# Moving first-norm statistics from attention into the convolution stages, and lending three heads in place of two to accumulating transfers

## The chip, the cores and the metric

The kernel runs on one core of one Trainium2 chip. The metric is the device time of one execution in microseconds (us). Names of engines: PE is the matrix engine (PEld its weight loads), DVE the vector engine, ACT the activation engine, POOL the general-purpose engine, SP the engine that only issues transfers. Each engine works through its own instructions in order, and waits on semaphores for the others.

## What is computed

Four images of 256 channels and 48 x 48 pixels pass two layers in fp32. Cut to what matters:

```python
def layer0(x):                     # x: (4, 256, 48, 48)
    y = relu(batchnorm(conv3x3(group_norm(x))))          # "first norm" is this group_norm
    q, k, v = split(einsum('oc,bchw->bohw', qkv_w, y))   # 8 heads of 32 channels, N = 2304 tokens
    attn = softmax(einsum('bhdn,bhdm->bhnm', q, k) * 32 ** -0.5)
    return x + proj(einsum('bhem,bhnm->bhen', v, attn))

def layer1(x):
    g = group_norm(x)                                    # second norm
    w = conv3x3(g, 45 maps)                              # 5 dilations x 9 taps, softmax over taps
    cat = [g] + [sum_taps(g shifted by dilation d, weighted by w) for d in (1, 6, 12, 24, 36)]
    return x + batchnorm_over_batch(conv1x1(cat))
```

A group norm needs the mean and the variance of each group of 8 channels over the whole image before any of it can be normalized.

## The kernel before

**Stages.** An image's 256 channels are two halves of 128 partitions. The loop over `b` from 0 to 4 makes one round per image: the convolution with q, k and v of image `b` (`conv_qkv`), side by side with the dynamic filters (layer 1) of image `b - 1` (`dynamic_filters`), and then attention of image `b` (`attention`). So the time line is: convolution of image 0 alone, attention 0, filters 0 with convolution 1, attention 1, filters 1 with convolution 2, attention 2, filters 2 with convolution 3, attention 3, filters 3 alone, the end. In the shared stages a planner with a cost clock (`clock`, `fill`, `run`) decides at build time how the matmuls of the two are interleaved; in attention the order is written out by hand. The order of the program on each engine is fixed.

**Attention.** It goes over 9 units of queries (eight of 512 queries of one half, that is 4 heads each, and a ninth that takes the last 256 queries of both halves), and in each unit over 18 key blocks `m` of 128 keys. In one step (`scores`, L954 to L963) PE makes the scores of 4 heads, one into a PSUM tile `so` with one buffer and three into `se` with two, and ACT takes their exponentials into a tile `p` of 4 x 512 numbers per partition (L962 one head, L963 three). In the next step (`weigh`) PE multiplies `p` with v into `num` (L983), and the sum of `p` over the key blocks is kept in `acc`, from which the denominator is made in `close` two units later (L1015, L1024, L1026, L1027, L1034). `p` has four buffers: the exponential of step m + 4 must wait until everything that reads `p` of step m is done.

**Lent key blocks.** The sum is DVE's (L999, all four heads). In units 1 to 8, in the steps m of `LENT = (2, 5, 8, 11, 14)` (the last unit leaves out 14), DVE adds two heads only, and POOL issues a transfer of the other two from `p` into `extra`, a slice of the tile `scratch`: a plain copy for m = 2 (L1001), and one that adds to what is there for the others (L1003). Each of these transfers waits for the one before. At the unit's last step (m = 15 in the last unit) DVE adds `extra` to `acc` (L1006). The tile `scratch` is 1536 numbers wide, of which 1024 are used.

**Projections.** In step 6 of units 3, 5, 7 and 8 finished parts of the attention output are projected (`project`, L1069, and L1078 and L605 on DVE), one part of six in units 3, 5 and 8, two in unit 7, the sixth after attention. `project` writes a tile `pp` of the same PSUM pool as `se`.

**Statistics of the next image.** The class `Norm` makes them in three parts: `part` is one `bn_stats` of DVE (L605) for each of 12 pieces; `finish` is a generator: first `bn_aggr` (L614), then a small matmul (L617), a copy and two squares on ACT (L618, L620), then two more matmuls (L627, L628) and `rstd_of` (DVE L87, a square root on ACT L88, DVE L89); `shift_of` is one DVE instruction (L634). Exponential and square root are in different tables of ACT, so a square root costs two table loads, there and back. `stats_of` loads the 12 pieces of image `b + 1` by SP (`xst`, L1516) and calls `part`; it is advanced by `merged` within the convolution of image `b`. The three parts of `finish` are in a list `spare`, called by attention of image `b` in step 2 of unit 1 and just ahead of the projections of units 3 and 5, with the third bank of `pp` for the small matmuls. Behind them in `spare` are three calls that normalize image `b + 1` in place (12 instructions of ACT, L1734, in three groups of 4): two calls in unit 7, one in unit 8.

Of the kernel before, what the change touches and what calls it, by code (L numbers as in the profile page):

```python
# [33 lines left out]
QC = 512  # L34
# [14 lines left out]
def conv_preact_kernel(  # L49
# [482 lines left out]
    with tc.tile_pool(name="w", bufs=1) as wpool, tc.tile_pool(  # L532
# [394 lines left out]
        def attention(b, q, k_, vT, pools, spare, project, scratch):  # L927
# [4 lines left out]
            zeros = work0.tile([P, D], F32, tag="zeros", name=f"zeros_{b}", bufs=1)  # L932
            nc.gpsimd.memset(zeros, 0.0)

            extra = scratch[:, : 2 * QC].rearrange("p (j n) -> p j n", j=2)
            scratch = work0.tile([P, QC], F32, tag="rt", name=f"rt_{b}", bufs=1)

            whole, rest = N // QC * QC, N % QC
# [30 lines left out]
            def weigh(u, m, p):  # L969
                if m == 0:  # L970
                    state[u] = dict(
                        num=ps_a.tile([P, 512], F32, tag="num", name=f"num_{b}_{u}"),
                        acc=work0.tile([P, 4, QC], F32, tag="acc", name=f"acc_{b}_{u}"),
                    )
                st = state[u]
                several = len(units[u]) > 1
                if several and m == 0:

                    for j, r in enumerate(heads):
                        nc.tensor.matmul(st["num"][r, :], zeros, p[:, j, :], start=True, stop=False)  # L980
                for i, (g, q0, n, at) in enumerate(units[u]):
                    for j, r in enumerate(heads):
                        nc.tensor.matmul(  # L983
                            st["num"][r, at : at + n],
                            vT[:, m, g * P + j * D : g * P + (j + 1) * D],
                            p[:, j, at : at + n],
                            start=(m == 0 and not several),
                            stop=(m == NT - 1 and i == len(units[u]) - 1),
                        )
                end = u == last  # L990
                if end and m == NT - 1:
                    sums(u, p, True, False)
                elif m == 0:
                    st["first"] = p
                else:
                    other = st["first"] if m == 1 else st["acc"]
                    lend = u > 0 and m in LENT[: len(LENT) - end]
                    js = slice(0, 2 if lend else 4)
                    nc.vector.tensor_tensor(st["acc"][:, js], other[:, js], p[:, js], ALU.add)  # L999
                    if lend and m == LENT[0]:  # L1000
                        nc.gpsimd.dma_start(out=extra, in_=p[:, 2:])  # L1001
                    elif lend:
                        nc.gpsimd.dma_start(out=extra, in_=p[:, 2:], accum_op=ALU.add)  # L1003
                if u and m == (NT - 3 if end else NT - 1):
                    rest = st["acc"][:, 2:]
                    nc.vector.tensor_tensor(rest, rest, extra, ALU.add)  # L1006
                if m == NT - 1 and not end:
                    g, q0, n, _ = units[u][0]
                    nc.scalar.copy(ao[:, g, q0 : q0 + n], st["num"])
# [29 lines left out]
            for i, (u, m) in enumerate(steps):  # L1039
                ps = scores(u, m)  # L1040


                if m == 1 and u > 1:
                    close(u - 2)
                if prev is not None:
                    weigh(*steps[i - 1], prev)
                prev = ps
                if m == 2 and u == last:
                    close(u - 1)
                if m == 6 and (u % NH == 1 or u == last):  # L1050
                    while (chunk + 1) * CH <= units[u if u == last else u - 1][0][1]:
                        pp = three(f"pp_{b}_{chunk}")
                        if spare:
                            spare.pop(0)(pp[:, 2, :])
                        project(chunk, ao, pp)
                        chunk += 1
                if m == 2 and u == 1 and spare:
                    spare.pop(0)(None)
            assert not spare
            weigh(*steps[-1], prev)  # L1060
            close(last)
# [42 lines left out]
            for _, _, _, y0, y1, x0, x1 in taps_of(c, n)  # L1104
        )

        def dynamic_filters(b, ao, chunk, norm, other, pools):


            ps_w, ps_y, ps_m, work1 = pools  # L1110
# [6 lines left out]
            def run(ns):  # L1117

                while ns > 0:
                    got = next(other, None)  # L1120
                    if got is None:
                        return
                    spent[0] += got
                    ns -= got
# [98 lines left out]
            ready = {}  # L1223


            while chunk < NCK:
                project(b, chunk, ao, ps_y.tile([P, 2, 512], F32, tag="y", name=f"pp_{b}_{chunk}"), norm)
                chunk += 1
            table(AF.Sqrt)
            run(2400)  # L1230
            for at, _ in enumerate(norm.finish(misc)):
                run((600, 700)[at])
            table(AF.Exp)

            for r0, r1 in ((0, 2 * R + 1), (2 * R + 1, HH)):
# [348 lines left out]
                    nc.sync.dma_start(out=image_of(out, b)[:, :, cols], in_=ty[c])  # L1584

        u_next = None
        for b in range(B + 1):

            with tc.tile_pool(name=f"work1_{b}", bufs=2) as work1, tc.tile_pool(
# [11 lines left out]
                if b < B:  # L1601
                    weights, between = taken, ()
                    if b == 0:
                        wc = work1.tile([P, NH, 9, C], F32, tag="wc", name="wc", bufs=1)
                        for h in range(NH):
                            nc.gpsimd.dma_start(out=wc[:, h], in_=conv_w[:, h])
                        nc.gpsimd.dma_start(out=wqkv, in_=qkv_w)
                        nc.gpsimd.dma_start(out=wp, in_=proj_w)
                        nc.gpsimd.dma_start(out=vbc, in_=v_b.rearrange("(h p) -> p h", p=P))
                        nc.gpsimd.dma_start(out=wcat, in_=cat_w)  # L1610
                        nc.gpsimd.dma_start(out=wsc, in_=scale_w)
                        weights = Made(wc, work1)
                        rest = norm0.finish(psc)
                        next(rest)
                        weights.pair(ORDER[0], [0], weights.home)
                        for _ in rest:
                            pass
                        norm0.shift_of()
                        def rows(r0, r1):
                            for h in range(NH):  # L1620
                                to, of = (
                                    inside(pads[0], h, r0, r1 - r0),
                                    rows_of(x_first[:, h, :])[:, r0:r1, :],
                                )
                                if h:
                                    nc.scalar.activation(
                                        to, of, AF.Identity, bias=norm0.shift[:, h : h + 1],
                                        scale=norm0.rstd[:, h : h + 1],
                                    )
                                else:  # L1630
                                    normalize(to, of, norm0.mean, norm0.rstd, h)


                        rows(0, HH // 2 + 2)
                        weights.pair(ORDER[0], [1], weights.home)
                        between = (
                            lambda: rows(HH // 2 + 2, HH),
                            lambda: weights.pair(3, range(NH), weights.other),
                        )
                        u_next = weights(ORDER[0])  # L1640
                    nn, stats = None, iter(())
                    if b + 1 < B:
                        nn = Norm("n0", b + 1)
                        stats = stats_of(b + 1, work1, nn)
                    other = merged(
                        conv_qkv(b, pads[b % 2], psc, weights, u_next, work1, between), 40000.0,
                        4000.0, stats,
                    )
                if b == 0:
                    for j, _ in enumerate(other):  # L1650
# [15 lines left out]
                else:  # L1666
# [31 lines left out]
                            for c, t in enumerate(y_2):  # L1698
                                nc.sync.dma_start(out=t, in_=chunk_of(y_d, 2, c))

                    dynamic_filters(b - 1, ao, chunk, norm1, other, (ps_w, ps_y, ps_m, work1))
                    if b == B:
                        finish(work1)
            if b == B:
# [13 lines left out]
            if b + 1 < B:  # L1718
                load_pad(b + 1)
                u_next = taken(ORDER[0])  # L1720
                bank = [None]
                fin = nn.finish(lambda name, bank=bank: bank[0])

                def stats(t, nn=nn, bank=bank, fin=fin):
                    bank[0] = t
                    if next(fin, fin) is fin:
                        nn.shift_of()

                todo = [(h, r0) for h in range(NH) for r0 in range(0, HH, R)]

                def pieces(_, some, b=b, nn=nn):
                    for h, r0 in some:
                        t = inside(pads[(b + 1) % 2], h, r0, R)
                        nc.scalar.activation(  # L1734
# [1 line left out]
                            scale=nn.rstd[:, h : h + 1],  # L1736
                        )

                spare = [stats] * 3 + [
                    lambda t, some=todo[i::3], f=pieces: f(t, some) for i in range(3)  # L1740
                ]
            norm1 = Norm("n1", b)
            q, k_, vT = qkv[b]
            with tc.tile_pool(name=f"work0_{b}", bufs=2) as work0, tc.tile_pool(
# [81 lines left out]
```

## Time and profile before

| | us |
|---|---|
| median of 3 runs (lowest, highest) | 2887.96 (2886.28, 2889.66) |
| the profiled execution | 2887.44 |
| its span, first to last instruction | 2885.7 |
| convolution of image 0, up to the first exponential | 0 to 145.3 |
| exponentials of attention 0, 1, 2, 3 (first and last start) | 145.3 to 511.8, 836.7 to 1204.7, 1529.6 to 1897.1, 2217.3 to 2580.9 |
| busy PE, DVE, ACT, POOL | 2726.2, 2445.6, 1677.0, 1190.2 |
| granted PE clock, mean | 0.979 |

A row of the groups names a line of the code, the engine, the operation, what is written and read, how often, the busy time in all, the mean of one, and then the time for which the engine stood idle just before such instructions, with what ended the wait. A row of the timeline gives start, duration, engine, line and operation, and in brackets the idle time before. L962 starts each step of attention, so the distance between two starts of L962 is the length of a step.

### The profile page before, as it was taken

Reading aid. Unit: us, or ns where it says so; the run is one execution under the profiler, and the core shown is the slowest. Engines: PE = TensorE matmul, PEld = TensorE weight load, DVE = VectorE, ACT = ScalarE, POOL = GpSimd, SP = SyncE. Lnnn points to the kernel's source line nnn. Section 1 sums busy time; section 2 is a strip of 40 time slices with the busy share of each in tenths; the row PEclk is TensorE's granted clock in tenths of the full one; section 3 lists DMA queues with packets and bytes.
Section 4 is the critical chain, followed back from the end, with each engine's and each line's share of the span. In section 5 each row is a group of like instructions: output and inputs, shape, how many; then the busy total and the mean of one; then the engine's idle time right before and its main releaser. Section 6 shows DMA issues by size and latency. Waiting matters only on the chain. (4 is left out here: it accounts for less than half of the span.)

```text
span 2885.7 us, 43628 instructions
## 1 busy us (share of the span) xinstructions
PE 2726.2 (94%) x16950; PEld 1202.4 (42%) x16950; DVE 2445.6 (85%) x2570; ACT 1677.0 (58%) x2107; POOL 1190.2 (41%) x1000
## 2 busy tenths in 40 slices
PE   7999999999999999999899999999999999998994
PEld 5722224556542222456562222356555222244562
DVE  6489999789879989878887998978886999987886
ACT  3398988322359889712237988842234988861224
POOL 1000000898840000299791010069986011006893
PEclk9999999999999999999999999999999999999997
DMA  4413333122242233223224333323213133325225
GB/s 179 104 31 71 67 65 82 44 89 87 68 104 64 65 72 76 61 64 95 68 68 99 67 72 72 70 55 87 69 50 77 45 72 76 73 50 222 60 70 207
DMA packets 148199, 232.04 MB, mean 80 GB/s; under 512 B 66760, under 2 KB 117008, under 8 KB 146192
## 3 DMA queue, kind: packets, MB, share of 16 engines
q0 software_dynamic: 23264, 87.21, 13.5%
q1 hardware_dynamic: 82384, 87.31, 10.7%
q10 hardware_dynamic: 42336, 54.66, 7.0%
q8 instruction: 135, 2.21, 0.3%
q14 instruction: 80, 0.66, 0.1%
HBM read 115.02 MB, written 32.33 MB: 51 GB/s over the span
## 5 line engine op out<-in xcount | busy, mean ns | idle before, releaser
L999 DVE TENSOR_TENSOR acc<-acc,p 128x2048 f32<-128x2048 f32 (+1 forms) x572 | 1144.2, 2000 | 59.9 <-ACT p L963 3.2
L1477 POOL TENSOR_TENSOR cat<-cat,prod 128x752 f32<-128x752 f32 (+9 forms) x661 | 883.0, 1345 | 145.8 <-DVE prod L1460 109.2
L963 ACT ACTIVATE p<-se 128x1536 f32<-128x1536 f32 x648 | 938.4, 1448 | 0.0
L954 PE MATMUL se<-q,k 32*128 32x512 f32 (+1 forms) x4320 | 738.9, 594 | 0.1
L954 PE MATMUL so<-q,k 32*128 32x512 f32 (+1 forms) x1440 | 730.6, 595 | 8.9 <-DVE bound L922 6.0
L983 PE MATMUL num<-p,vT 128*32 128x512 f32 (+1 forms) x5760 | 703.5, 561 | 4.2 <-ACT p L963 2.4
L1460 DVE TENSOR_TENSOR prod<-wb,pad 128x384 f32<-128x384 f32 (+8 forms) x687 | 483.1, 738 | 91.1 <-POOL cat L1477 51.8
L962 ACT ACTIVATE p<-so 128x512 f32<-128x512 f32 x648 | 388.5, 600 | 183.8 <-PE se L954 81.5
L954 PEld LDWEIGHTS so<-q,k 32*128 32x128 f32 x1440 | 216.6, 183 | 524.9 <-ACT p L962 478.4
L1003 POOL DMA_DIRECT2D scratch<-p x124 | 105.6, 852 | 770.6 <-ACT p L963 732.1
L1287 PE MATMUL py<-cat,wsc 128*128 128x384 f32 x960 | 349.7, 494 | 9.7 <-POOL cat L1477 8.3
L1400 ACT COPY wb<-ws 128x384 f32<-128x384 f32 (+3 forms) x260 | 121.7, 468 | 366.9 <-DVE prod L1460 232.3
L983 PEld LDWEIGHTS num<-p,vT 128*32 128x32 f32 x5760 | 131.4, 108 | 480.0 <-issue 446.8
L1403 PE MATMUL wb<-w,pick 128*128 128x384 f32 (+3 forms) x628 | 300.3, 510 | 22.2 <-DVE prod L1460 13.0
L1001 POOL DMA_DIRECT2D scratch<-p x32 | 17.9, 559 | 572.4 <-ACT p L963 521.7
L954 PEld LDWEIGHTS se<-q,k 32*128 32x128 f32 x4320 | 227.5, 183 | 5.5 <-ACT p L963 4.1
L1287 PEld LDWEIGHTS py<-cat,wsc 128*128 128x128 f32 x960 | 176.5, 192 | 114.3 <-POOL cat L1477 24.5
L1403 PEld LDWEIGHTS wb<-w,pick 128*128 128x128 f32 x628 | 116.8, 191 | 136.0 <-DVE prod L1460 58.1
L851 PE MATMUL pc<-cv_q,u 128*128 128x288 f32 x576 | 160.3, 412 | 7.3 <-DVE cv_q L742 6.5
L1139 PE MATMUL pg<-pad,wcat 128*45 128x384 f32 x864 | 158.8, 499 | 2.1 <-DVE pad L592 2.0
L851 PE MATMUL pc<-cv_k,u 128*128 128x288 f32 x576 | 156.6, 410 | 3.7 <-ACT m L797 2.0
L884 PE MATMUL pq<-hid,wqkv 128*128 128x384 f32 x384 | 138.0, 499 | 11.8 <-DVE yt L786 11.8
(233 smaller groups left out, 2308.7 us busy)
## 6 DMA issues: line engine op xcount, KB each, us to landing
scratch<-p POOLq DMA_DIRECT2D x156, 512.0 KB, 4.4
ws<-w_d ACTq DMA_DIRECT2D x256, 192.0 KB, 3.1
pad<-in_x SPq DMA_DIRECT2D x14, 1152.0 KB, 15.1
u<-u_d SPq DMA_DIRECT2D x18, 768.0 KB, 4.7
x_d<-pad SPq DMA_DIRECT2D x48, 192.0 KB, 2.5
xst<-in_x SPq DMA_DIRECT2D x36, 192.0 KB, 2.4
y_d<-y SPq DMA_DIRECT2D x15, 384.0 KB, 3.3
u_d<-u SPq DMA_DIRECT2D x6, 768.0 KB, 3.7
```

The source lines that it names most:

```text
L851: nc.tensor.matmul(m, u[:, h, kx, o * P : (o + 1) * P], halves[g][:, h, i, :, kx : kx + WW], start=(h == 0 and kx == 0), stop=(h == NH - 1 ...
L884: nc.tensor.matmul(pq[:, :CH], wqkv[:, i, s, g * P : (g + 1) * P], hid[:, i, cols], start=(i == 0), stop=(i == NH - 1),)
L954: nc.tensor.matmul(dst[:, at : at + n], k_[r, g, m * P : (m + 1) * P], q[r, g, q0 : q0 + n], start=True, stop=True,)
L962: nc.scalar.activation(p[:, 0, :], s1, AF.Exp, scale=QS)
L963: nc.scalar.activation(p[:, 1:, :], s3, AF.Exp, scale=QS)
L983: nc.tensor.matmul(st["num"][r, at : at + n], vT[:, m, g * P + j * D : g * P + (j + 1) * D], p[:, j, at : at + n], start=(m == 0 and not s ...
L999: nc.vector.tensor_tensor(st["acc"][:, js], other[:, js], p[:, js], ALU.add)
L1139: nc.tensor.matmul(pg[64 * s : 64 * s + NG, :CH], wcat[:, ii, k, :], window(gn, ii, cc * R, k // 3 - 1, k % 3 - 1), start=(i == 0 and k == 0),
L1287: nc.tensor.matmul(to, wsc[:, n * NH + i, o * P : (o + 1) * P], rhs(i), start=(n == 0 and i == 0), stop=(last and i == NH - 1),)
L1403: nc.tensor.matmul(pw[:, : nr * WW], pick[:, k : k + 1].to_broadcast([P, P]), w[:, l0 * WW : l1 * WW], start=True, stop=True,)
L1460: nc.vector.tensor_tensor(pv, wb, src, ALU.mult)
L1477: nc.gpsimd.tensor_tensor(dst, dst, pv, ALU.add)
```

## The change

The statistics of image 1 and of image 2 are now both made during the convolution of image 0 (24 pieces; `merged` advances them every 2000 ns of planned time there and no longer every 4000), those of image 3 during the convolution of image 1, and none during the convolution of image 2. `finish` and `shift_of` of image 1 stand in the convolution of image 0, between two loads of ACT's tables. Those of image 2 and image 3 stand at the start of the filters of image 0 and image 1 (the generator `beside`), next to the same steps of the second norm, and share its table loads. Attention has none of it any more; the 12 normalizing instructions of ACT are split into five groups (3, 3, 2, 2, 2), and are called with the projections of units 3, 5, 7 (twice) and 8.

In attention DVE now adds one head in a lent step and the transfer takes three (768 KB in place of 512 KB), `extra` is the whole of `scratch`, and L1006 adds three heads.

The diff, without unchanged surroundings:

```diff
-            extra = scratch[:, : 2 * QC].rearrange("p (j n) -> p j n", j=2)
+            extra = scratch.rearrange("p (j n) -> p j n", j=3)
...
-                    js = slice(0, 2 if lend else 4)
+                    js = slice(0, 1 if lend else 4)
                     nc.vector.tensor_tensor(st["acc"][:, js], other[:, js], p[:, js], ALU.add)
                     if lend and m == LENT[0]:
-                        nc.gpsimd.dma_start(out=extra, in_=p[:, 2:])
+                        nc.gpsimd.dma_start(out=extra, in_=p[:, 1:])
                     elif lend:
-                        nc.gpsimd.dma_start(out=extra, in_=p[:, 2:], accum_op=ALU.add)
+                        nc.gpsimd.dma_start(out=extra, in_=p[:, 1:], accum_op=ALU.add)
                 if u and m == (NT - 3 if end else NT - 1):
-                    rest = st["acc"][:, 2:]
+                    rest = st["acc"][:, 1:]
                     nc.vector.tensor_tensor(rest, rest, extra, ALU.add)
...
                         pp = three(f"pp_{b}_{chunk}")
                         if spare:
-                            spare.pop(0)(pp[:, 2, :])
+                            spare.pop(0)()
                         project(chunk, ao, pp)
                         chunk += 1
-                if m == 2 and u == 1 and spare:
-                    spare.pop(0)(None)
...
-        def dynamic_filters(b, ao, chunk, norm, other, pools):
+        def dynamic_filters(b, ao, chunk, norm, other, pools, beside):
...
+            next(beside, None)
             while chunk < NCK:
                 project(b, chunk, ao, ps_y.tile([P, 2, 512], F32, tag="y", name=f"pp_{b}_{chunk}"), norm)
                 chunk += 1
             table(AF.Sqrt)
             run(2400)
             for at, _ in enumerate(norm.finish(misc)):
+                if at:
+                    next(beside, None)
                 run((600, 700)[at])
+            for _ in beside:
+                pass
             table(AF.Exp)
...
-                    nn, stats = None, iter(())
-                    if b + 1 < B:
-                        nn = Norm("n0", b + 1)
-                        stats = stats_of(b + 1, work1, nn)
+                    def first_norms():
+
+                        for i in (1, 2) if b == 0 else (b + 2,):
+                            if i < B:
+                                norms[i] = Norm("n0", i)
+                                yield from stats_of(i, work1, norms[i])
+                            if i == 1:
+                                table(AF.Sqrt)
+                                yield from finished(1)
+                                table(AF.Exp)
+
+                    def finished(i):
+                        yield from norms[i].finish(psc)
+                        norms[i].shift_of()
+
+                    stats = first_norms()
                     other = merged(
                         conv_qkv(b, pads[b % 2], psc, weights, u_next, work1, between), 40000.0,
-                        4000.0, stats,
+                        4000.0 if b else 2000.0, stats,
                     )
...
-                    dynamic_filters(b - 1, ao, chunk, norm1, other, (ps_w, ps_y, ps_m, work1))
+                    dynamic_filters(
+                        b - 1, ao, chunk, norm1, other, (ps_w, ps_y, ps_m, work1),
+                        finished(b + 1) if b + 1 < B else iter(()),
+                    )
...
-                spare = [stats] * 3 + [
-                    lambda t, some=todo[i::3], f=pieces: f(t, some) for i in range(3)
-                ]
+                spare = [lambda some=todo[i::5], f=pieces: f(some) for i in range(5)]
```

More of the change, by code (lines that the diff above doesn't have):

```diff
@@ L1586, in conv_preact_kernel @@
         u_next = None
+        norms = {}
         for b in range(B + 1):
@@ L1720, in conv_preact_kernel, with pieces @@
                 u_next = taken(ORDER[0])
[L1721 to L1727, printed above, removed]
                 todo = [(h, r0) for h in range(NH) for r0 in range(0, HH, R)]
-                def pieces(_, some, b=b, nn=nn):
+                def pieces(some, b=b, nn=norms[b + 1]):
                     for h, r0 in some:
```

## The prediction

> **What bounds the kernel now.** I read the page first (shares, groups), then the timeline of single attention steps, the waits, and the windows of the stages.
>
> ```profile
> PE 2726.2 (94%) x16950; PEld 1202.4 (42%) x16950; DVE 2445.6 (85%) x2570; ACT 1677.0 (58%) x2107; POOL 1190.2 (41%) x1000
> ```
>
> PE is at 94%, so only PE's idle time can be won. The groups, shapes apart, name what attention needs per step:
>
> ```profile
> L999 DVE TENSOR_TENSOR acc<-acc,p 128x2048 f32<-128x2048 f32 x416 | 953.3, 2292 | 43.4 <-ACT p L963 1.9 <-DVE acc L999 0.5
> L962 ACT ACTIVATE p<-so 128x512 f32<-128x512 f32 x648 | 388.5, 600 | 183.8 <-PE se L954 81.5 <-PE so L954 28.8 <-DVE acc L999 13.9
> L999 DVE TENSOR_TENSOR acc<-acc,p 128x1024 f32<-128x1024 f32 x156 | 190.9, 1224 | 16.5 <-ACT p L963 1.4
> L1006 DVE TENSOR_TENSOR acc<-acc,scratch 128x1024 f32<-128x1024 f32 x32 | 39.2, 1225 | 1.1
> ```
>
> L962 waits mostly for PE, for DVE only 13.9 us in the whole kernel. An undisturbed step is 2.07 us from one L962 to the next, PE working without a gap and the product with v starting 0.04 us after L963 ends: ACT has no slack there, and a late `p` buffer holds PE one for one. Now what the moved statistics cost. First image 0 at the projection of unit 5, then image 3 in unit 3, where there is no next image:
>
> ```profile
> 356.56 0.38 PE L627 MATMUL pp<-mvn,gmat 128*128 128x2 f32 x2
> ...
> 357.61 1.28 ACT L88 ACT_TABLE_LOAD   x1
> 358.79 0.15 DVE L87 TENSOR_SCALAR grstd_n<-pp 128x2 f32<-128x2 f32 x1
> ...
> 359.00 4.54 PE L1069 MATMUL pp<-ao,wp 128*128 128x384 f32 x8 [1.83 <-DVE grstd_n L87]
> 359.20 1.28 ACT L962 ACT_TABLE_LOAD   x1
> ```
>
> ```profile
> 2349.04 2.85 PE L1069 MATMUL pp<-ao,wp 128*128 128x384 f32 x8
> ...
> 2352.97 0.60 ACT L962 ACTIVATE p<-so 128x512 f32<-128x512 f32 x1 [2.91 <-PE se L954]
> ```
>
> PE does the tiny matmuls, waits for DVE's L87, which stands behind a sum, and even the projection is slower. In image 3 ACT idles 2.91 us there. The transfers:
>
> ```profile
> 2357.27 0.86 POOL L1003 DMA_DIRECT2D scratch<-p  x1 [8.35 <-ACT p L963]
> ```
> ```profile
> 2363.32 0.60 ACT L962 ACTIVATE p<-so 128x512 f32<-128x512 f32 x1
> ```
> ```profile
> q8 instruction: 135, 2.21, 0.3%
> ...
> scratch<-p POOLq DMA_DIRECT2D x156, 512.0 KB, 4.4
> ```
>
> The L962 shown overwrites the buffer that this transfer reads, 6.05 us after its issue; it lands in 4.4. The stages with filters and convolution:
>
> ```profile
> 1206.80:1529.60 322.80, 302.64 (x1209) 186.95 (x1208) 259.61 (x407) 83.47 (x167) 284.05 (x217) 0.98 0.26 71
> 1899.20:2217.30 318.10, 301.09 (x1209) 186.40 (x1209) 253.22 (x396) 83.30 (x168) 284.41 (x217) 0.98 0.23 65
> ```
>
> Columns after the time: PE, PEld, DVE, ACT, POOL. They differ in the 12 `bn_stats` and loads of the next image; the second has none and is 4.7 us shorter.
>
> **What the Trainium skill says.** *ScalarE: Activation LUTs*, section "What ACT_TABLE_LOAD costs", puts a switch at 1283 ns and a drain of 1380 ns; the trace agrees on 1283 and shows no drain as long as that (load at 357.61, square root at 358.98). *DMA: Bandwidth & Descriptors*, "SDMA does more than copy", limits an adding element run to 2048; 1536 is below, so one packet per partition should stay one. No run here shows it. The same page, "Queues, rings and completion order": each DMA engine goes round its queues packet by packet. *Runtime: NRT & Kernel Launch*, "Instruction fetch mechanics": instructions come in blocks of 16 KiB by DMA. The trace agrees: 135 packets of 16384 bytes, most about 0.99 us long, share the engines with `p`.
>
> **The change part by part.** The sum is against the profiled execution, 2887.44 (span 2885.7 and 1.7 around it).
>
> *Statistics out of attention.* Step 6 of unit 3 lasts 5.98 us in images 0 to 2 and 4.85 in image 3; of unit 5, 8.97, 9.32, 8.98 against 4.84. Gain 3 x 1.13 + 4.13 + 4.48 + 4.14 = **-16.1**. The new normalizing calls there are 3 x 0.60 us (starts of L1734 are 0.60 apart), inside ACT's 2.9 us of idleness, so nothing; without that cover 1.8 us each. Units 7 and 8 show it: their step 6 is as long with 8 and 4 calls as in image 3 without.
>
> *Convolution 2 without statistics*: **-4.7** (322.8 - 318.1; 12 x 0.55 us of DVE and 12 loads on SP leave it).
>
> *Convolution 0 with 12 more pieces.* DVE is half idle there (74.7 of 146 us), so 12 x 0.55 hide. On SP 12 loads of 192 KB go ahead of later stores of `u`, for which nobody waits for hundreds of us. POOL's memset ahead of attention already waits for the last `bn_stats`, which stays earlier than the convolution's end. On PE: three tiny matmuls, 0.9 us with their loads. They take one of two PSUM buffers at the change from conv to qkv: I count a wait for yt's read (0.5), one for ACT's copy of the first q (0.8), and one where the second copy (k) stands on ACT behind square root and table load, 2.3 us less two matmul groups' cover (0.7). **+3.0**, between 1 and 6.
>
> *Starts of filters 0 and 1.* The two `bn_aggr` (0.28 each) fit into DVE's wait for the projection (5.4 us at 521 us). Ahead of the normalization L592, for which PE waits with the 45-map convolution (already 1.6 us per image by the waits of L1139), DVE gets L87, the wait for the second square root, L89 and L634: 0.15 + 0.3 + 0.17 + 0.16 and four gaps, about 0.8; PE waits 0.3 for ACT's squares. Two stages by 1.1 = **+2.2** (1 to 4).
>
> *DVE relieved.* From 2292 and 1224 ns an addition costs 1.04 ns per number and 157 ns: 690 for one head (the 128x512 addition L1034 takes 692), about 1760 for three. A unit saves 5 x 0.53 - 0.53 = 2.1 us of DVE, 66 us in the kernel. Most of it is nothing, since DVE hides behind PE. What shows: DVE starts a sum 3.2 us after `p` is ready at the start of a unit and 1.1 to 1.9 at its end. Only where the buffer of step 0 is due for step 4 does L962 wait for it: units then last 38.8 us, and 38.58 in the two where it does not. With DVE 0.6 us earlier at the unit's start (1.16 of lag gone, the longer L1006 taken off) I count 0.1, 0.43, four times 0.25, and 0.2 for units 1 to 7, and 0.5 in unit 8, where `se` waits for L1024 behind DVE: 2.2 per image, **-9.0**. At the end of attention PE waits for the last sum; it comes 0.5 earlier: **-2.0**.
>
> *Longer transfers.* In the trace's packet records an adding transfer is 128 packets of 4096 bytes, 8 per DMA engine, 331 ns each; a plain one takes 159 for 4096 and 234 for 6144 bytes. So 331 = 2 x 159 + 13 gives 481 at 6144, proportion gives 496. The last semaphore write comes 4.12 us after issue; 8 x 0.16 later is 5.39. L962 starts 0.38 us after that write where it waits, so the limit is 6.05 - 0.38 = 5.67: 0.28 us to spare, no undisturbed transfer stalls. But where a 16 KiB instruction fetch falls into the first 1.1 us of packets, one engine is late: 11 of 124 adding transfers land at about 5.6; 8 more are met at their start (4.4 to 5.7, about 0.7 late). After the change those land near 6.85 and 6.1: stalls of 1.2 and 0.45. The window grows by half: 108 transfers have no other slack (27 per image), so 108 x 11/124 x 1.5 = 14 by 1.2, and 7 by 0.45: 20, less 1.2 lost already, about **+18** (8 to 30).
>
> Sum: -16.1 - 4.7 + 3.0 + 2.2 - 9.0 - 2.0 + 18 = -8.6, so 2878.8 for the profiled execution; the median of the runs is 0.5 above it: **2879.3**.
>
> **Rivals.**
> *Transfers stay hidden.* If a fetch delays an engine no longer than now relative to the 6.05 us, the +18 is +3: 2864. For it: the spare 0.28 is positive; against: landings of 5.7 today leave 0.0 for 1.3 us more.
> *Each transfer stalls (slower).* Place: L962 of step m + 4, and POOL's next issue, which waits for the same transfer. From 522 ns per packet on every adding transfer holds ACT; at 560 (0.3 us) 108 x 0.3 = 32, with fetches 25: 2888 - 26.6 + 57 = 2918. It decides above about 532 ns per packet: (26.6 - 18)/108 = 0.08 us. For it: no adding packet of that size is in the trace, and 40 ns separate me from the limit; against: the plain ones are linear.
> *DVE's relief is worth little* because the units' first steps (2.29, 2.72, 2.53) are set by `den` taking a PSUM buffer: 3 us in place of 11: 2887, no change.
>
> **How the numbers follow.** Forecast 0.50 (its own range 2872 to 2887), hidden 0.15, each stalls 0.20, little relief 0.15. A measurement tells about 0.2% (5.8 us) from nothing. Faster: three quarters of the forecast and all of "hidden", 0.53; same: 0.12 of the forecast, 0.11 of little relief, 0.03 of the slower case, so 0.26 or 0.27; slower 0.20. The range from 2863 to 2900 leaves out half of the stalling case, a third of the hidden one and some tails: about 2 in 10.
>
> **What would show it.** Step 6 of units 3 and 5 at 4.85 in all images. The second shared stage near 319 us. Adding packets at 480 to 500 ns and landings of 5.4. Units of 38.6 us, but about 20 steps of 3 us and more, L962 waiting for the transfer. Convolution 0 some 3 us longer. I am wrong if L962 waits for most transfers, or if late landings don't stall.

## The result, and the profile after

The change makes no difference that this comparison can tell: median 2884.69 us (2880.97 to 2885.45, 4 runs) beside 2887.12 for the kernel before on the same chip, a ratio of 0.999 (95% interval 0.9973 to 1.0007). A later repeat with 21 runs puts it at 2883.88 beside 2887.73, ratio 0.9984 (0.9977 to 0.999): 0.16% faster, 3.9 us. The prediction was 2879.3 with a range of 2863 to 2900. The profiled execution took 2885.45 us with a span of 2883.7; before it was 2887.44 and 2885.7.

A difference of 2 to 4 us is what is left of several larger ones that nearly cancel. First the shares and the groups of the kernel after, shapes apart (busy time and mean of one, then the idle time ahead and what ended it):

```profile
PE 2721.6 (94%) x16950; PEld 1199.6 (42%) x16950; DVE 2381.2 (83%) x2570; ACT 1671.8 (58%) x2105; POOL 1187.6 (41%) x1000
```
```profile
L962 ACT ACTIVATE p<-so 128x512 f32<-128x512 f32 x648 | 388.4, 599 | 198.1 <-PE se L954 84.7 <-DMA scratch<-p 29.0 <-PE so L954 26.9
L999 DVE TENSOR_TENSOR acc<-acc,p 128x512 f32<-128x512 f32 x156 | 108.0, 692 | 16.1 <-ACT p L962 0.5
L1003 POOL DMA_DIRECT2D scratch<-p x124 | 105.6, 852 | 766.7 <-ACT p L963 571.1 <-DMA scratch<-p 172.8 <-ACT p L962 22.8
L1006 DVE TENSOR_TENSOR acc<-acc,scratch 128x1536 f32<-128x1536 f32 x32 | 56.3, 1758 | 1.1
```

DVE was relieved as planned: 692 ns for one head and 1758 ns for three, 64 us less busy time. But L962, which waited for DVE for 13.9 us before, now waits for the transfers for 29.0 us. POOL's idle time that the landing of the transfer ahead ended went from 11.5 us to 172.8 (POOL has little else to do in attention, so this counts how often it was held, not what was lost). The list of all waits has the sum, how often, and the longest; first before, then after:

```profile
ACT p L962 <- DVE acc L999: 13.9, 34, 0.8
...
POOL scratch L1003 <- DMA scratch<-p: 11.5, 2, 5.8
...
PE den L1015 <- DVE acc L999: 7.6, 4, 1.9
...
ACT p L962 <- DMA scratch<-p: 0.9, 2, 0.5
```
```profile
POOL scratch L1003 <- DMA scratch<-p: 172.8, 29, 7.4
...
ACT p L962 <- DMA scratch<-p: 29.0, 32, 1.9
...
ACT p L962 <- DVE acc L999: 5.2, 13, 0.5
...
PE den L1015 <- DVE acc L999: 3.5, 4, 1.4
```

The row of `den` is PE's wait for the last sum at the end of each attention; it fell by 4.1 us in all. The statistics went from attention as they should. The timeline of image 0 at the projection of unit 5 (start, duration, instruction, idle time before; L1067 was L1069 before the change, L1745 was L1734):

```profile
357.35 0.60 ACT L962 ACTIVATE p<-so 128x512 f32<-128x512 f32 x1
...
358.26 2.85 PE L1067 MATMUL pp<-ao,wp 128*128 128x384 f32 x8
359.18 1.90 ACT L1745 ACTIVATE pad<-pad,gshift_n,grstd_n 128x384 f32<-128x384 f32 x3
```

Where PE made small matmuls, waited 1.83 us for L87 and took 4.54 us for the projection, it now takes 2.85 us at once, and the three normalizing instructions stand inside ACT's idle time. Six steps later in the same unit comes a loss:

```profile
366.50 0.85 POOL L1003 DMA_DIRECT2D scratch<-p  x1 [8.13 <-ACT p L963]
...
373.97 0.60 ACT L962 ACTIVATE p<-so 128x512 f32<-128x512 f32 x1 [1.55 <-DMA scratch<-p]
374.39 0.85 POOL L1003 DMA_DIRECT2D scratch<-p  x1 [7.04 <-DMA scratch<-p]
...
374.62 0.69 PE L954 MATMUL so<-q,k 32*128 32x512 f32 x1 [1.09 <-ACT p L962]
```

A transfer tells of its end by 16 packets of 4 bytes, the semaphore writes, which the trace's packet records hold. The transfer issued at 366.50 makes the last of them 7.08 us later; ACT, then PE, stand until then, and so does POOL's next transfer. The same transfer in the page's list of DMA issues (KB, median from issue to landing; 512.0 KB and 4.4 us before), the DMA queue of POOL before and after (packets, MB, share), and the windows of the second and third shared stage (first exponential after last exponential; PE, PEld, DVE, ACT, POOL):

```profile
q0 software_dynamic: 23264, 87.21, 13.5%
```
```profile
q0 software_dynamic: 23264, 128.10, 19.5%
...
scratch<-p POOLq DMA_DIRECT2D x156, 768.0 KB, 5.7
```
```profile
1205.00:1521.30 316.30, 300.30 (x1215) 186.61 (x1207) 252.72 (x399) 83.95 (x171) 283.20 (x217) 0.99 0.25 65
1892.60:2209.70 317.10, 300.97 (x1209) 186.20 (x1209) 252.27 (x395) 83.29 (x167) 283.44 (x217) 0.98 0.24 65
```

The queue has as many packets as before (23264), so a partition's 6144 bytes stay one adding packet, as the Trainium skill (*DMA: Bandwidth & Descriptors*, "SDMA does more than copy") had let me expect. The second stage no longer differs from the third.

The starts of L962 split the kernel into parts. In us, from the profiled executions:

| | before | after |
|---|---|---|
| convolution of image 0 | 145.3 | 146.7 |
| attention, four images, first to last L962 | 1465.5 | 1468.1 |
| ... beyond 2.07 per step, units 1 to 8: steps 0 to 2 | 46.1 | 46.1 |
| ... steps 3 to 5 (waits for DVE) | 9.9 | 1.5 |
| ... step 6 (projections, statistics) | 71.1 | 54.9 |
| ... steps 7 to 17 (transfers) | 1.0 | 26.9 |
| shared stages | 325.0, 324.9, 320.2 | 325.6, 318.5, 319.2 |
| filters of image 3 and end | 304.8 | 305.6 |

So units 1 to 8 of attention won 16.2 + 8.4 us and lost 25.9 to the transfers. The waits of `den` at the ends of attention lie in the rows below it, 0.6, 1.4, 1.1 and 1.1 us less after the change.

### The profile page after: what moved, and what is told of

Same layout as the page of the kernel before. It is cut to its first block, busy times and chain, and to the rows that moved or that the text cites. A ratio compares the mean times of both kernels' runs of the same rounds, so it can differ in the third digit from the quotient of the medians.

```text
span 2883.7 us, 43644 instructions
## 1 busy us (share of the span) xinstructions
PE 2721.6 (94%) x16950; PEld 1199.6 (42%) x16950; DVE 2381.2 (83%) x2570; ACT 1671.8 (58%) x2105; POOL 1187.6 (41%) x1000
## 3 DMA queue, kind: packets, MB, share of 16 engines
q0 software_dynamic: 23264, 128.10, 19.5%
## 5 line engine op out<-in xcount | busy, mean ns | idle before, releaser
L999 DVE TENSOR_TENSOR acc<-acc,p 128x2048 f32<-128x2048 f32 (+1 forms) x572 | 1061.2, 1855 | 116.3 <-ACT p L963 66.5
L963 ACT ACTIVATE p<-se 128x1536 f32<-128x1536 f32 x648 | 938.5, 1448 | 0.0
L962 ACT ACTIVATE p<-so 128x512 f32<-128x512 f32 x648 | 388.4, 599 | 198.1 <-PE se L954 84.7
L1003 POOL DMA_DIRECT2D scratch<-p x124 | 105.6, 852 | 766.7 <-ACT p L963 571.1
L884 PE MATMUL pq<-hid,wqkv 128*128 128x384 f32 x384 | 136.6, 494 | 11.5 <-DVE yt L786 11.2
```

The source lines that it names most:

```text
L884: nc.tensor.matmul(pq[:, :CH], wqkv[:, i, s, g * P : (g + 1) * P], hid[:, i, cols], start=(i == 0), stop=(i == NH - 1),)
L962: nc.scalar.activation(p[:, 0, :], s1, AF.Exp, scale=QS)
L963: nc.scalar.activation(p[:, 1:, :], s3, AF.Exp, scale=QS)
```

## The experiments

Every ratio is to the kernel before, on the same chip, with its 95% interval. "Excess" means the time beyond 2.07 us per step, as in the table, and "..." stands for lines that a diff leaves out (the size of `extra` follows the number of heads that the transfer carries).

**Statistics alone.** The change, but with two heads lent as before:

```diff
-                    js = slice(0, 1 if lend else 4)
+                    js = slice(0, 2 if lend else 4)
...
-                        nc.gpsimd.dma_start(out=extra, in_=p[:, 1:])
+                        nc.gpsimd.dma_start(out=extra, in_=p[:, 2:])
...
-                        nc.gpsimd.dma_start(out=extra, in_=p[:, 1:], accum_op=ALU.add)
+                        nc.gpsimd.dma_start(out=extra, in_=p[:, 2:], accum_op=ALU.add)
...
-                    rest = st["acc"][:, 1:]
+                    rest = st["acc"][:, 2:]
```

> The statistics moved as in the change, but two heads lent as before. Theory A (the statistics win what I predicted, and the long transfers give it back): step 6 of units 3 and 5 at 4.85 us (-16.1), the second shared stage about 6 us shorter, convolution 0 about 1.4 longer, everything else as before: 2887 - 21 = 2866, ratio 0.993. L962 waits for transfers about 1 us in all. Theory B (the statistics' gain was lost elsewhere, in the convolution of image 0 and at the starts of the filters): 2880 or more, ratio above 0.9975.

Measured 2866.97 us, ratio 0.9928 (0.9914 to 0.9942): 19.7 us faster than the kernel before. Step 6 has 55.0 us of excess (71.1 before), steps 7 to 17 have 3.0, and L962 waits for DVE nearly as before:

```profile
L962 ACT ACTIVATE p<-so 128x512 f32<-128x512 f32 x648 | 388.9, 600 | 179.9 <-PE se L954 79.8 <-PE so L954 25.6 <-DVE acc L999 11.2
```

This half of the change is the good one, and alone it is some 17 us better than the whole.

**Lending alone.** The kernel before, with three heads lent:

```diff
-                    js = slice(0, 2 if lend else 4)
+                    js = slice(0, 1 if lend else 4)
...
-                        nc.gpsimd.dma_start(out=extra, in_=p[:, 2:], accum_op=ALU.add)
+                        nc.gpsimd.dma_start(out=extra, in_=p[:, 1:], accum_op=ALU.add)
```

> Three heads lent as in the change, statistics as before. Theory A: waits for transfers some 25 us more, DVE's relief some 9 to 11 us less, so slower by 14 to 18: 2903, ratio 1.005 to 1.0065. Theory B (the lending itself is about even, and the statistics are too): 2885 to 2888, ratio 1.000.

Measured 2891.07 us, ratio 1.001 (1.0002 to 1.0018): 4.4 us slower, not 14 or more. The excess of steps 7 to 17 is 26.0, so the transfers cost what they cost in the change. What I had not expected is step 6: 61.6 us in place of 71.1, although the statistics are still there. The timeline of image 0, unit 5, of this kernel:

```profile
357.42 0.15 DVE L87 TENSOR_SCALAR grstd_n<-pp 128x2 f32<-128x2 f32 x1
357.58 1.28 ACT L88 ACT_TABLE_LOAD   x1
357.62 2.85 PE L1069 MATMUL pp<-ao,wp 128*128 128x384 f32 x8 [0.48 <-DVE grstd_n L87]
```

The kernel before has L87 at 358.79 and PE waiting 1.83 us for it, and the projection then takes 4.54. PE's small matmuls start at the same time (356.56 there, 356.54 here); a DVE with less to add answers 1.4 us earlier. The step lasts 5.93, 6.28 and 5.70 us in images 0 to 2 (8.97, 9.32, 8.98 before, 4.84 to 4.85 without statistics). Each half of the change removes these same 9.5 us of waiting, so their gains don't add: 19.7 alone and -4.4 alone would be 15.3 together, and 2 to 4 were measured. Another 1.9 us of steps 3 to 5 is counted twice in the same way (9.9 before, 8.0 with the statistics alone, 1.6 with the lending alone).

**DVE relieved, transfers short.** DVE adds one head in a lent step, but the transfer still carries two; the lent blocks of the second of the four heads are left out of the sum, so this kernel's times stand for the relief without its price. (Its closing addition, of two heads, is 0.53 us shorter than the change's, so the relief is a little larger than there.)

```diff
                     js = slice(0, 1 if lend else 4)
...
-                        nc.gpsimd.dma_start(out=extra, in_=p[:, 1:], accum_op=ALU.add)
+                        nc.gpsimd.dma_start(out=extra, in_=p[:, 2:], accum_op=ALU.add)
```

> The changed kernel, but the transfers carry two heads while DVE adds one in lent steps and the closing addition takes two (the sum of the lent blocks of one head is left out): DVE's relief without the longer transfers. Theory A: 9 to 13 us below the kernel with the statistics alone, units of 38.6 us: 2855, ratio 0.989. Theory C (the first steps of a unit are set by PSUM buffers and PE, so DVE's lag costs nothing): equal to the kernel with the statistics alone, 2866.

Measured 2857.74, ratio 0.9896 (0.9881 to 0.9912), 9.2 us below the kernel with the statistics alone. The excess of steps 3 to 5 goes from 8.0 to 1.5, that of steps 7 to 17 is 2.6.

```profile
L962 ACT ACTIVATE p<-so 128x512 f32<-128x512 f32 x648 | 388.3, 599 | 168.8 <-PE se L954 75.3 <-PE so L954 23.7 <-DVE acc L999 5.2
```

**Long transfers, DVE not relieved.** The transfer carries three heads, DVE still adds two, and the closing addition takes only the two other heads of the transfer; the third is carried for nothing.

```diff
-                    js = slice(0, 1 if lend else 4)
+                    js = slice(0, 2 if lend else 4)
...
-                    rest = st["acc"][:, 1:]
-                    nc.vector.tensor_tensor(rest, rest, extra, ALU.add)
+                    rest = st["acc"][:, 2:]
+                    nc.vector.tensor_tensor(rest, rest, extra[:, 1:], ALU.add)
```

> The changed kernel, but DVE adds two heads as before and the closing addition takes two of the three heads that the transfers carry: the longer transfers without DVE's relief. Theory A: L962 waits some 25 us more for transfers than in the kernel with the statistics alone, about 2890, ratio 1.001, so 5 to 10 above the changed kernel. Theory C: as the changed kernel, 2884.

Measured 2883.44, ratio 0.9986 (0.9979 to 0.9992): 16.5 us above the statistics alone. In steps 7 to 17 the length of the transfers by itself costs 23.0 us (3.0 to 26.0), nearly all that was lost there. L962 waits for them as in the change:

```profile
L962 ACT ACTIVATE p<-so 128x512 f32<-128x512 f32 x648 | 388.5, 600 | 198.3 <-PE se L954 84.8 <-DMA scratch<-p 27.2 <-PE so L954 24.9
```

But I had expected some 2890, since here DVE has as much to do as before. Steps 3 to 5 have only 2.9 us of excess (8.0 with short transfers). While ACT and PE stand for a late transfer, DVE goes on, and begins the next unit without a backlog. The units bear this out: of units 2 to 8, the 20 that follow a unit with a stall in its last eight steps have 0.02 us of this excess on average, the other 8 have 0.24; with the statistics alone it is 0.00 (5 units) against 0.33 (23). Once the transfers stall, relieving DVE is worth about nothing (2883.4 without it, 2883.9 and 2884.7 with it); where they don't, it is worth 9 us.

**A fifth buffer for `p`.** If L962 loses its time because the transfer still reads the buffer that it wants, a fifth buffer gives the transfer another step of about 2.07 us. If the chain of transfers, each waiting for the one ahead, or the traffic itself were the cause, it would change little. To make room, the weights of the 1x1 convolution, held in SBUF throughout, are loaded again in each stage that uses them. That alone, with four buffers, is the base:

```diff
-        wsc = wpool.tile([P, (1 + len(DILATIONS)) * NH, C], F32, tag="wsc", name="wsc")
...
+                if b > 0:
+                    wsc = work1.tile(
+                        [P, (1 + len(DILATIONS)) * NH, C], F32, tag="wsc", name=f"wsc_{b}", bufs=1
+                    )
+                    nc.sync.dma_start(out=wsc, in_=scale_w)
...
-                        nc.gpsimd.dma_start(out=wsc, in_=scale_w)
```

> The changed kernel with the 1x1 weights no longer kept in memory through attention but loaded again at the start of each filter stage (four loads of 1.5 MB on SP): makes room, changes nothing in attention. It is the base of the next kernel. Both theories: 0 to 5 us above the changed kernel, 2885 to 2890, with the same waits of L962 for transfers (25 to 30 us).

Measured 2882.98, ratio 0.9979 (0.9971 to 0.9986), within 2 us of the change and 2 below what I expected, with the same waits (lines are one less in this kernel and the next two: L961 is L962, L962 is L963, L1002 is L1003):

```profile
ACT p L961 <- DMA scratch<-p: 28.6, 32, 2.1
```

Then, on top of it:

```diff
-                p = work0.tile([P, 4, QC], F32, tag="p", name=f"p_{b}_{u}_{m}", bufs=4)
+                p = work0.tile([P, 4, QC], F32, tag="p", name=f"p_{b}_{u}_{m}", bufs=5)
```

> As the kernel with the reloaded weights, and the room used for a fifth buffer of p, so that a buffer is due 2.07 us later. Theory A (the loss is L962's wait for the buffer that a late transfer still reads): L962's waits for transfers go below 4 us, steps 7 to 17 of the units back to 2.07, about 25 us less than the kernel with reloaded weights: 2860 to 2864, ratio 0.991. Theory D (the loss comes from the chain of transfers, each waiting for the one before on POOL, or from the traffic itself slowing other accesses): less than 8 us gained, 2877 or more.

Measured 2856.81, ratio 0.9889 (0.9874 to 0.9904), 26.2 us below its base, 31 below the kernel before and 27 to 28 below the change, with nothing of the computation left out. That is 3 to 7 us better than I had expected. The groups:

```profile
L961 ACT ACTIVATE p<-so 128x512 f32<-128x512 f32 x648 | 388.3, 599 | 168.1 <-PE se L953 53.8 <-PE so L953 26.7 <-issue 23.1
...
L1002 POOL DMA_DIRECT2D scratch<-p x124 | 105.6, 852 | 769.2 <-ACT p L962 551.4 <-DMA scratch<-p 114.4 <-ACT p L961 103.4
```

L961 waits for transfers no more, and steps 7 to 17 have 0.5 us of excess (26.2 in the base), while POOL still waits for the transfer ahead (114.4 us, 19 times). The transfers are as long, and 41 of 124 are still late (last write over 5.5 us after issue; 36 in the change); ACT and PE no longer stand for them. So nearly the whole loss of these steps was the wait for a free `p`.

**Five buffers, two heads lent.** The kernel before this, lending two heads again. It asks whether the third head is worth anything once the buffer is there:

```diff
-                    js = slice(0, 1 if lend else 4)
+                    js = slice(0, 2 if lend else 4)
...
-                        nc.gpsimd.dma_start(out=extra, in_=p[:, 1:], accum_op=ALU.add)
+                        nc.gpsimd.dma_start(out=extra, in_=p[:, 2:], accum_op=ALU.add)
```

> The kernel with five p buffers and two heads lent. Theory A: with two heads only 1 to 4 us were lost to late transfers, but the fifth buffer also removes L962's waits for DVE (8 to 11 us in step 4 and around), so about as fast as the one with three heads and five buffers, within 4 us: 2860 to 2866. Theory D: as the kernel with the statistics alone plus the reload, 2867 to 2872.

Measured 2865.65, ratio 0.9924 (0.991 to 0.9937). This lies within the times that I gave, but I had also expected it within 4 us of the one before, and it is 8.8 above. L961 waits for DVE's sums no more here:

```profile
L961 ACT ACTIVATE p<-so 128x512 f32<-128x512 f32 x648 | 388.5, 600 | 171.6 <-PE se L953 73.0 <-PE so L953 30.4 <-DVE ao L1033 2.3
```

Still, steps 3 to 5 keep 5.8 us (1.3 with three heads), 3.3 of them in unit 8, and PE waits 7.7 us for the last sums at the ends of attention (5.4 with three heads). So the fifth buffer does not take over all that the relief of DVE gives. Of the 7.3 us between the two profiled executions 3.5 lie in attention and 2.3 in those waits at its ends; for the rest no place was found.

**The change again**, beside these on one chip:

> The changed kernel once more beside the others on one chip: 2884, ratio 0.999. Its profile shows whether the same transfers are late again: theory A says that the instruction fetches sit at nearly the same places of the program, so about 30 late transfers and 21 us of stalls again.

Measured 2883.88, as told above. The transfers are late in the same places: all 36 that are late in the change are late here (38 in all), and 34 of the 36 stalls are in the same steps. Steps 7 to 17 have 24.5 us (26.9), the wait of L962 for them is 25.4 us, 30 times, and POOL's 165.9. The lateness belongs to the program, not to chance.

## Why the prediction was right where it was, and wrong where it wasn't

The time lay in the range, 4.6 to 5.4 us above the forecast. That by itself says little: the range is 37 us wide and holds gains and losses, and of the 8 us that I had forecast as gain 2 to 4 came. By the terms of the sum, on the profiled executions:

- *Statistics out of attention, -16.1*: right. Step 6 fell by 16.2 us in the change and by 16.1 with the statistics alone, to 4.85 us in units 3 and 5, as in image 3 before. The normalizing calls cost nothing there.
- *Convolution 2 without statistics, -4.7*: right. The stage fell by 6.4 us in this pair and by 4.2 with the statistics alone; without the wait of `den` at its start (1.4 and 0.2) that is 5.0 and 4.0.
- *Convolution 0, +3.0*: +1.4, and +0.2 with the statistics alone. All eight profiled executions with the statistics moved take 145.3 to 146.9 us there, the two without 145.3 and 143.9, so +3.0 was probably too much. Which of the waits that I counted one by one are covered was not looked at.
- *Starts of filters 0 and 1, +2.2*: right in sum. PE's own wait for L592 went from 2.0 to 4.5 us; in filters 0 and 1 it rose by 2.3, but by 2.15 in filters 0 and by 0.1 in filters 1, not by 1.1 in each.
- *DVE relieved, -9.0*: -8.4 in steps 3 to 5, and 9.2 us in time where DVE was relieved with short transfers. The size is right; the *independence* of this term was not. Lent alone, it takes another 9.5 us out of the statistics' step, and beside stalling transfers it is worth nothing, since they let DVE catch up anyway. The first of these could not show in the change, where the statistics are gone from there.
- *End of attention, -2.0*: PE's waits for the last sum (`den`) fell by 4.1 us, from 7.6 to 3.5. With five buffers, where no transfer stalls, they are 5.4, so 2.2 less: the relief itself is worth what I had put. The rest came with the stalls, in which DVE catches up.
- *Longer transfers, +18*: **the term that was mis-sized**, though within its range of 8 to 30; steps 7 to 17 lost 25.9 us (1.0 to 26.9). The price of one transfer was right: adding packets of 6144 bytes take 481 ns (481 to 496 predicted), and the last semaphore write comes 5.33 us after the issue (5.39). The limit of 5.67 leaves an undisturbed one 0.34 us. What was missing are two kinds of lateness, below.

So a miss of 8 us in the last term was in part made up by small ones on the other side (some 2 us each in convolution 0 and at the ends of attention). That part is luck.

By transfers, from the packet records of the change: of 124 adding ones 36 make their last semaphore write later than 5.5 us after issue, and each of them has a packet of an instruction queue beside it, of 16384 bytes for 34 and of 8192 for two. Three kinds of stall make nearly all of the 26.9 us:

1. A fetch met within the packets: 19 transfers, with writes between 5.9 and 7.4 us after issue, and 15 stalls, 17.2 us. This is what I predicted, 14 by 1.2 and 7 by 0.45, so 20 us. The first data packet starts 1.43 us after issue. In 11 of the 19 the fetch runs already then, which was my second class; here the 11 stall for 6.7 us. The 16 fetches that still run at the issue but end before that first packet delay nothing (15 writes by 5.36; the one at 5.52 has an 8192-byte packet beside it).
2. A fetch whose packet starts together with the last write, 5.5 to 5.9 us after issue, up to half a microsecond late: 16 stalls, 6.2 us (in two of them it is the 8192-byte packet). The write itself is not what is slow: in the 14 others the last two data packets in a row ahead of it take some 1.5 us together where two others take 0.96, and the fetch's own packet starts only as the second ends. I had left this class out; before the change its writes were late by some 0.15 us and had 1.5 us to spare.
3. Transfers that POOL itself issued late, by 1.1 to 1.6 us after `p` was complete instead of 0.29, though the transfer ahead had landed: three places, 2.6 us. The same three transfers were as late in the kernel before (1.03 to 1.57), inside the old slack. Why POOL is late there the trace doesn't show.

Together 26.0 of 26.9. That a fetch is the cause in the first two kinds rests on their coincidence in the trace, and in the first on the size of the delay (last section); no run moved the fetches. That the stall comes from the buffer is shown by the fifth one.

The rivals: *transfers stay hidden* fell with 29.0 us of waiting. *Each transfer stalls* fell with 481 ns; its threshold was 532. *DVE's relief is worth little* fell as a statement on the relief (9.2 us), but the change ended within a few us of the 2887 that it gave, by another way.

## What to carry to other kernels

Before a transfer is lengthened, compare its *latest* landing, not its usual one, with the moment when its buffer is wanted again: 0.34 us of slack looked enough, and with 36 of 124 transfers disturbed it cost more than the engine it relieved gave back. Here a buffer more was worth 26 us where the relieved engine was worth 9, and it kept both gains. And two edits that take load from the same wait (here a tiny reply of DVE in the middle of PE's step) must be priced together, in both orders.

## What the runs showed of the hardware

- An adding transfer within SBUF takes 331 ns per packet of 4096 bytes and 481 per 6144; plain ones 159 and 234. POOL spends 852 ns on issuing it and 559 on a plain one.
- Instruction fetches of 16384 bytes delay a transfer whose packets they meet by 0.5 to 2.05 us (19 transfers of the change). The Trainium skill (*DMA: Bandwidth & Descriptors*, "Queues, rings and completion order") has each DMA engine take its queues in turn, a packet at a time; if a packet record of the trace is such a packet, which no run shows, a fetch should cost what is left of its own. Where the fetch already runs when the first data packet starts, the trace agrees: in 9 of 11 transfers the delay is what is left then, less about 0.1 us (0.53 us for 0.63 left, 1.73 for 1.83), and in 11 of 12 in the repeat. Where it starts in the midst of the transfer, over half a microsecond after the first packet, it costs more: 1.46 to 2.05 us for fetches of 0.96 to 0.99 (four transfers).
- Where a fetch's packet starts together with the last semaphore write, the two data packets in a row ahead took some 1.5 us together in place of 0.96, and the write was late by about 0.5 us (14 transfers of the change).
- A stall of ACT and PE is not lost for everybody: with the long transfers and DVE not relieved, 26 us of it took 5 us out of the waits for DVE.
